# A graph-attention kernel: weights transposed first, a shorter last table store, and weighing steps moved among the logits steps near the end

## The chip, the cores and the metric

One core of a Trainium2 chip runs the kernel. The metric is the time of one execution on the device in microseconds (us), the median of several runs. Engines: TensorE (PE, with PEld for its weight loads), VectorE (DVE), ScalarE (ACT), GpSimd (POOL), SyncE (SP). An engine works through its instructions in the order in which the program emits them and waits on semaphores for the others. SP, ACT and POOL also issue DMAs, on queues named SPq, ACTq and POOLq.

## The reference

3125 nodes with 128 features, 100000 edges sorted by destination, five edge types `r`, eight heads of 16. For each type, an edge's logit per head is query times key, the softmax runs over the edges of that type into one node, and the values are summed with it:

```python
q = einsum('eh,khd->ekd', x_dst, W_Q[r]); k = ...x_src, W_K[r]; v = ...x_src, W_V[r]
logits = (q * k).sum(-1) / scale + attn_bias[r]
masked = where(mask, logits, NEG)
exp_l = where(mask, exp(masked - segment_max(masked, dst)[dst]), 0.0)
out += segment_sum((exp_l / (segment_sum(exp_l, dst)[dst] + 1e-12))[:, :, None] * v, dst)
# after the types
h = out @ out_proj_w.T + out_proj_b + x
x = layernorm(x + layernorm(h) * ln_gamma + ln_beta)
```

Only the edges of type `r` count for `r`, so every edge is worked on once, with the weights of its own type.

## The kernel before, in words

The nodes lie in 25 blocks of 128 (the last has 53), the edges in 196 groups of 512. A group is a tile of 128 partitions by 4 edges, and its edges go to at most 25 neighbouring nodes, that is 125 rows (node, type) of a window. The whole work is in `windowed_path`; `general_path` is a fall-back for other inputs and does not run here. The Tile framework is told to keep the order in which instructions are emitted (`manual_schedule`), so the order of the Python code is the order of each engine's queue.

**Start.** Weights, node features and edge lists are loaded. The first node of each group (`fr`) is copied to floats (`frf`), spread to all partitions by a matmul with `ones` (`fp`, `firsts`) and turned into `first`, `first5` and part of `nkey`. Then the weights are transposed on PE in four quarters (`d0` = 0, 4, 8, 12) into two PSUM buffers `wp`, and copied out to `wkv` and `wq` by DVE and ACT. A loop over the 25 blocks makes the table of keys and values: `turn(b)` transposes a block of features, `table(b)` multiplies it with `wkv` (three matmuls), copies the result to one of three buffers `kvs` and stores it to `kv_d` in DRAM, 128 nodes x 5 types x 256 floats, 640 KB. Between tables the loop runs the pieces in `side`: `rows_of` finds the rows of the edge list in which a node's edges begin, `in_row` fetches them (POOL), `count` counts (ACT), `keys_a` to `keys_c` and `along` build the indices, `checks` tests the input's form.

**Steps.** The rest is one loop over steps `k`, written as a hand-made software pipeline. Per group: `gather` fetches the 512 table rows with four indirect DMAs on POOL into one of 24 buffers `kv`; `fetch` loads the group's keys `kt` and window of queries `qw` (SP); `spot` makes a one-hot matrix `hot` (DVE); `spread_q` brings the queries to the edges (12 bf16 matmuls); `logits` multiplies and reduces (DVE, lines 613 and 614); `store_logits` writes them to `lg_d`. At step `k` group `k` has its logits.

Once all edges of a block have logits, `maxima_load` fetches, for each node, 64 edges from the block's place in `lg_d` into `ell` (one indirect DMA on POOL), and `maxima` (ACT copies `ell` to `by_head`, DVE adds masks and reduces) works out the maxima in two parts, three types and then two; `store_m` writes them. From `LAG` = 8 steps after the block's last logits on, its groups can be weighed: `fetch_m`, `spread_m` (12 small matmuls, `me`), `less_max` (DVE), `exps` (ACT), `weigh` (DVE, line 707), `places` (ACT: the one-hots `at` of destinations, five Abs at line 719 and one Relu at line 722), `sums` (PE, fp32, lines 733 to 743), `carry` (ACT), `norm` (DVE), `by_node` (ACT). The table `at_k` gives the step in which a group `v` is weighed:

```python
for v in range(NGR):
    k = max(k + 1, full_at(block_of(v), D) + LAG)
    at_k[v] = k
```

It runs 19 steps behind the logits from `v` = 22 on. So logits end at step 195, and steps 196 to 214 hold weighing only. When a block is complete, `project` (PE) and `residual` (DVE) come at `done_at` and one step later, `roots` (a square root on ACT, which needs another activation table than the exponential) at `done_at` + 2 and `norms` (DVE) a step after that; `store_z` writes the block. `fetch_x` loads the residual's input `xr`; for the last, smaller block it first clears the buffer on DVE. The steps of blocks 19 to 24: roots at 186, 194, 201, 209, 217 and 220, the last normalisation at 222. Maxima of blocks 22, 23 and 24 are at steps 187/188, 195/196 and 198/199.

POOL's queue: gathers are emitted up to `AHEAD` = 3 groups ahead of the step, and a block's logits load follows the gathers of its step. SP's queue in each step: `fetch`, `fetch_x`, `store_z`, `store_m`, `store_q`, `fetch_m`, then `store_logits`.

Of the kernel before, what the change touches and what calls it, by code (L numbers as in the profile page):

```python
# [17 lines left out]
P = 128  # L18
# [3 lines left out]
R = 5  # L22
# [24 lines left out]
WR = WN * R  # L47
RH = 3
# [67 lines left out]
def windowed_path(  # L116
# [9 lines left out]
    kv_d = dram.tile([NP * R, KVW], F32, name="kv_d")  # L126
# [108 lines left out]
    five = iota("five", [[R, WN]], WN, mult=-1)  # L235
    ones = keep("ones", [P, P])
    nc.vector.memset(ones, 1.0)
    eps_t = keep("eps_t", [P, 1])
    nc.vector.memset(eps_t, LN_EPS)
# [14 lines left out]
    for b in range(NT):  # L254
# [4 lines left out]
    frf = load.tile([1, NGR + NSR], F32, name="frf")  # L259
    nc.vector.tensor_copy(frf, fr)  # L260
    fp = pps.tile([P, NGR + NSR], F32, name="fp", tag="tr", bufs=2)
    nc.tensor.matmul(fp, ones[0:1, :], frf, start=True, stop=True)
    firsts = load.tile([P, NGR + NSR], F32, name="firsts")
    nc.vector.tensor_copy(firsts, fp)
    nc.vector.tensor_copy(first, frf[:, :NGR])
    nc.vector.tensor_scalar_mul(first5, frf[:, :NGR], float(R))
    nc.vector.tensor_tensor(
        nkey[:, T, 1:], firsts[:, 1:NGR], firsts[:, : NGR - 1], op=ALU.subtract
    )
    nc.vector.tensor_scalar(  # L270
        nkey[:, T, 1:], nkey[:, T, 1:], float(R), row_of, op0=ALU.mult, op1=ALU.subtract
    )
    grp = load.tile([P, NT], F32, name="grp")
    grp_i = load.tile([P, NT], I32, name="grp_i")
    nodeh = load.tile([P, NT], F32, name="nodeh")
    nc.vector.tensor_scalar_add(nodeh, node, -0.5)
    into = load.tile([P, NT], F32, name="into")


# [3 lines left out]
    for d0 in range(0, HD, 4):  # L283
        wp = pps.tile([P, 4, 3, R, HEADS], F32, name="wp", tag="wp", bufs=2)
        for d in range(4):
            nc.tensor.transpose(
                wp[:, d].rearrange("h s r k -> h (s r k)"), wn[:, d0 + d :: HD],
                ident[: 3 * R * HEADS, : 3 * R * HEADS],
            )
        for s, (copy, to) in enumerate(  # L290
            ((nc.vector.tensor_copy, kv_to[:, 0]), (nc.scalar.copy, kv_to[:, 1]),
             (nc.vector.tensor_copy, q_to))
        ):
            copy(to[:, :, :, d0 : d0 + 4], wp[:, :, s].rearrange("h d r k -> h r k d"))

# [8 lines left out]
    def table(b, xT):  # L304
        kvs = work.tile([P, R * 2, H], F32, name="kvs", bufs=3)
        wf = wkv.rearrange("h r s c -> h (r s) c")
        for n, (c0, c1) in enumerate(((0, 4), (4, 8), (8, 10))):
# [9 lines left out]
            kv_d[b * P * R : (b + 1) * P * R, :].rearrange("(p r) c -> p (r c)", r=R),  # L317
            kvs.rearrange("p s h -> p (s h)"),
# [113 lines left out]
    def checks():  # L432
# [18 lines left out]
        0: [lambda: rows_of(0, 5)],  # L451
        1: [lambda: rows_of(5, 10)],
        2: [lambda: rows_of(10, 15)],
# [18 lines left out]
    for b in range(NT):  # L472
# [5 lines left out]
        while len(rows) < min(NT, 5 * b + 5) and len(rows) - counted < 8:  # L478
            rows[len(rows)] = in_row(len(rows))
# [53 lines left out]
    def fetch_x(name, b):  # L533
        n = min(P, N - b * P)
        xb = flow.tile([P, H], F32, name=name, bufs=2)
# [178 lines left out]
    def places(g):  # L714
# [3 lines left out]
        for t in range(n):  # L718
            nc.scalar.activation(  # L719
                at[:, t, :], row_at[:, :WR], AF.Abs, bias=nkey[:, t, g : g + 1], scale=1.0  # L720
            )
        nc.scalar.activation(at[:, :n, :], at[:, :n, :], AF.Relu, bias=1.0, scale=-1.0)  # L722
# [56 lines left out]
    def pair():  # L779
        return late_flow.tile([P, 2, nc.vector.BN_AGGR_DIM], F32, name="mv", bufs=2)  # L780
# [6 lines left out]
    def residual(b):  # L787
# [6 lines left out]
        h = late_flow.tile([P, H], F32, name="h")  # L794
# [9 lines left out]
    def norms(b):  # L804
        sd, mv = live.pop(("sd", b)), live.pop(("mv", b))
        nc.vector.reciprocal(sd, sd)
        if b < NT:
# [9 lines left out]
            live["mv", b + 1] = nxt = pair()  # L817
            nc.vector.memset(nxt, 0.0)
# [15 lines left out]

    at_k, k = {}, 0
    for v in range(NGR):
        k = max(k + 1, full_at(block_of(v), D) + LAG)
        at_k[v] = k
    v_at = {k: v for v, k in at_k.items()}
    done_at = {b: at_k[full_at(b)] + 4 for b in range(NT)}  # L840
    for b in range(1, NT):
        done_at[b] = max(done_at[b], done_at[b - 1] + 1)
    done_at[NT] = done_at[NT - 1] + 2
    norm_at = {b: d + (3 if b < NT - 1 else 2) for b, d in done_at.items()}

    q_at = [
        min(g for g in range(NGR) if min(block_of(g) + 1, NT - 1) >= b) - 3 for b in range(NT)
    ]
    q_from = []
    for b in range(NT):  # L850
        f = q_at[b] - 7
# [28 lines left out]
    for k in range(done_at[NT] + 4):  # L880
        v = v_at.get(k)
        q_step = {k - f: b for b, f in enumerate(q_from) if b not in first_b and -2 <= k - f <= 5}

        if k + 3 < NGR:
            fetch(k + 3)
        if -2 in q_step:
            fetch_x("xq", q_step[-2])
        for b in range(NT):
            if done_at[b] - 1 == k:
                fetch_x("xr", b)  # L890
            if norm_at[b + 1] + 1 == k:
                store_z(b)
            if full_at(b, D) + LAG - 3 == k:
# [3 lines left out]
        for u in range(NGR):  # L897
            if max(at_k[u] - 3, full_at(block_of(u), D) + LAG - 2) == k:
                fetch_m(u)

        while gathered < min(k + AHEAD, NGR - 1):
            gathered += 1
            gather(gathered)
        for b in range(NT):
            if full_at(b, D) + 1 == k:
# [20 lines left out]
        if k + 1 < NGR:  # L926
            spread_q(k + 1)
# [4 lines left out]
        if k + 1 < NGR:  # L932
            types(k + 1)
        if k < NGR:
            logits(k)
            store_logits(k)
# [4 lines left out]
        if k + 2 < NGR:  # L941
            spot(k + 2)
        if v_at.get(k + 1) is not None:
            places(v_at[k + 1])
# [4 lines left out]
        for b in range(NT):  # L949
            if full_at(b, D) + LAG - 5 == k:  # L950
                maxima(b, 0, RH)
            if full_at(b, D) + LAG - 4 == k:
                maxima(b, RH, R)
        for b in range(NT + 1):
            if done_at[b] + 2 == k:
                roots(b)
            if norm_at[b] == k:
# [514 lines left out]
```

## Time and profile before

| | |
|---|---|
| median of 3 runs | 1222.6 us (1218.9 to 1222.96) |
| profiled execution | 1219.8 us, its span 1218.0 us |
| busy, share of the span | PE 810.3 us (67%), PEld 701.4 (58%), DVE 928.8 (76%), ACT 750.5 (62%), POOL 804.9 (66%) |
| first and last gather, start | 100.3 and 1113.6 us |
| last logits, last weighing, start | 1118.8 and 1200.5 us |
| mean granted TensorE clock | 0.765 |

The profile is one execution. A slice row shows an engine's busy share in 40 equal parts of the span. A row of a timeline gives start and duration in us, engine, line, operation, tiles and shapes, how many rows were merged, and in brackets how long the engine was idle before and what ended that. In the window tables come the busy times of PE, PEld, DVE, ACT and POOL with counts, then the clock, the DMA engines' share and GB/s.

### The profile page before, as it was taken

The numbers are of one execution on the slowest core, as the hardware profiler recorded it, in microseconds if no ns is written. First come the engines' busy times: TensorE is split into PE (matmuls) and PEld (weight loads), VectorE is DVE, ScalarE is ACT, GpSimd is POOL, SyncE is SP. The second block draws the span as 40 slices with busy tenths as digits, with TensorE's granted clock in tenths as the row PEclk, the third lists the DMA queues.
The fourth block names the chain that finished last, engine by engine and source line by source line (L and its number), as shares of the span: only waits on it lengthen the run. The fifth ranks groups of instructions, "written<-read, shape, count | busy, mean of one in ns | idle before, by whom it ended". The sixth has DMA issues, their size and how long they took to land.

```text
span 1218.0 us, 25296 instructions
## 1 busy us (share of the span) xinstructions
PE 810.3 (67%) x7503; PEld 701.4 (58%) x7503; DVE 928.8 (76%) x2478; ACT 750.5 (62%) x2488; POOL 804.9 (66%) x902
## 2 busy tenths in 40 slices
PE   4793446657667766776667667766776686568584
PEld 2451235547656665665566656665665675567484
DVE  4751376777887898888888988888888889778744
ACT  1661015447656766776677667756766676667594
POOL 2705777777777777777777777777777777775000
PEclk9996566677777887887687778778877878777566
DMA  6984787667666767776776677667766776665000
GB/s 146 361 329 153 211 208 183 155 170 192 167 166 181 184 167 173 180 181 167 180 185 169 172 176 194 174 161 183 189 165 169 179 183 165 173 159 128 8 8 14
DMA packets 181138, 207.33 MB, mean 170 GB/s; under 512 B 82614, under 2 KB 145871, under 8 KB 180872
## 3 DMA queue, kind: packets, MB, share of 16 engines
q0 software_dynamic: 41392, 116.59, 34.5%
q1 hardware_dynamic: 135176, 84.34, 28.1%
q10 hardware_dynamic: 4424, 4.71, 1.5%
q8 instruction: 61, 1.00, 0.3%
q14 instruction: 85, 0.70, 0.2%
HBM read 169.90 MB, written 35.62 MB: 169 GB/s over the span
## 4 chain that ended last, share of the span: by engine, by line
DVE 31%; DMA 20%; POOL 14%; PE 13%; issue 11%; ACT 10%; SPq 1%; DVEq 0%; ACTq 0%; POOLq 0%
POOL kv L527 14%; DMA kv<-kv_d,idx 10%; DMA ell<-lg_d,start_i 5%; DVE prod L613 4%; DVE lg L614 4%; DVE wv L707 4%; PE pp L733 4%; DVE wl L653 3%; ACT at L719 3%; PE pr L309 3%; DVE mx L659 2%; DVE hot L591 2%; PE qe L600 2%; DVE den L756 1%; PE prq L553 1%
## 5 line engine op out<-in xcount | busy, mean ns | idle before, releaser
L527 POOL DMA_INDIRECT kv<-kv_d,idx x784 | 746.3, 952 | 274.2 <-issue 195.1
L733 PE MATMUL pp<-wv,at 128*125 128x136 f32 x1568 | 307.9, 354 | 17.0 <-DVE o L758 14.9
L719 ACT ACTIVATE at<-row_at,nkey 128x125 f32<-128x125 f32 x979 | 305.1, 390 | 0.0
L733 PEld LDWEIGHTS pp<-wv,at 128*125 128x125 f32 x1568 | 261.6, 243 | 25.4 <-DVE o L758 16.9
L600 PE MATMUL qe<-qw,hot 125*128 125x128 bf16 x2352 | 210.9, 254 | 31.1 <-DMA qw<-q_d 15.3
L600 PEld LDWEIGHTS <-hot 125*128 125x128 bf16 x2352 | 197.4, 124 | 36.8 <-DVE hot L591 21.4
L690 PE MATMUL me<-mw,hot 125*128 125x8 bf16 x2352 | 91.6, 168 | 184.5 <-DVE wv L707 116.0
L690 PEld LDWEIGHTS <-hot 125*128 125x128 bf16 x2352 | 84.3, 102 | 224.0 <-DVE wv L707 124.6
L707 DVE TENSOR_TENSOR wv<-kv,me 128x512 f32<-128x512 f32 x196 | 133.3, 680 | 76.1 <-ACT wv L702 74.0
L701 ACT ACTIVATE me<-me 128x32 f32<-128x32 f32 x196 | 36.3, 185 | 226.9 <-DVE me L697 225.8
L613 DVE TENSOR_TENSOR prod<-kv,qe 128x512 f32<-128x512 f32 x196 | 134.1, 684 | 33.7 <-PE qe L600 17.3
L722 ACT ACTIVATE at<-at 128x625 f32<-128x625 f32 (+1 forms) x196 | 142.2, 726 | 6.2
L614 DVE TENSOR_REDUCE lg<-prod 128x32 f32<-128x512 f32 x196 | 134.4, 686 | 6.8
L737 PE MATMUL pp<-pt,at 125*125 125x136 f32 x390 | 103.3, 355 | 33.9 <-ACT pt L749 33.7
L553 PE MATMUL prq<-wq,xTq 128*128 128x384 f32 (+1 forms) x100 | 59.4, 691 | 78.4 <-DVE rem L563 77.2
L737 PEld LDWEIGHTS pp<-pt,at 125*125 125x125 f32 x390 | 79.1, 246 | 41.2 <-ACT pt L749 40.6
L591 DVE TENSOR_SCALAR hot<-kt,row_of 125x512 bf16<-125x512 bf16 x196 | 73.5, 375 | 13.6 <-DMA kt<-key_d 13.4
L653 DVE TENSOR_TENSOR wl<-by_head,shut 128x1536 f32<-128x1536 f32 (+1 forms) x50 | 74.5, 1491 | 10.7 <-ACT by_head L638 9.8
L743 PEld LDWEIGHTS pp<-rsum,o 125*128 125x128 f32 x392 | 80.6, 250 | 1.7 <-ACT oT L768 1.4
L659 DVE TENSOR_REDUCE mx<-wl 128x24 f32<-128x1536 f32 (+1 forms) x50 | 74.3, 1486 | 1.7
L553 PEld LDWEIGHTS prq<-wq,xTq 128*128 128x128 f32 x100 | 22.6, 281 | 87.7 <-DVE rem L563 85.6
L743 PE MATMUL pp<-rsum,o 125*128 125x25 f32 x392 | 72.0, 267 | 1.4 <-DVE xr L537 1.3
(156 smaller groups left out, 992.9 us busy)
## 6 DMA issues: line engine op xcount, KB each, us to landing
kt<-key_d SPq DMA_DIRECT2D x196, 128.0 KB
qw<-q_d SPq DMA_DIRECT2D x196, 96.0 KB
kv_d<-kvs SPq DMA_DIRECT2D x25, 640.0 KB
kv<-kv_d,idx POOLq DMA_INDIRECT x784
q_d<-q SPq DMA_DIRECT2D x25, 480.0 KB
lg_d<-lg SPq DMA_DIRECT2D x196, 18.0 KB
mw<-m_d SPq DMA_DIRECT2D x196, 6.0 KB
xq<-in_x SPq DMA_DIRECT2D x24, 64.0 KB
```

The lines of the kernel that those rows point to most:

```text
L527: nc.gpsimd.indirect_dma_start(out=kv[:, t, :], out_offset=None, in_=kv_d[:, :], in_offset=bass.IndirectOffsetOnAxis(ap=idx[:, t, g : g + ...
L600: nc.tensor.matmul(qe[:, t, :], hot[:, t, :], qw[:WR, s, :], start=(s == 0), stop=(s == 2))
L613: nc.vector.tensor_tensor(prod, kv[:, :, :H], live.pop(("qe", g)), op=ALU.mult)
L614: nc.vector.tensor_reduce(lg[:, :, :HEADS], prod.rearrange("p t (k d) -> p t k d", d=HD), AX.X, ALU.add)
L653: nc.vector.tensor_tensor(wl[:, :n], by_head[:, None].to_broadcast([P, n, HEADS, D]), shut[:, :n, None, :].to_broadcast([P, n, HEADS, D]), ...
L690: nc.tensor.matmul(me[:, t, :], hot[:, t, :], mw[:WR, s, :], start=(s == 0), stop=(s == 2))
L707: nc.vector.tensor_tensor(wv[:, :, :H].rearrange("p t (k d) -> p t k d", d=HD), kv[:, :, H:].rearrange("p t (k d) -> p t k d", d=HD), live ...
L719: nc.scalar.activation(at[:, t, :], row_at[:, :WR], AF.Abs, bias=nkey[:, t, g : g + 1], scale=1.0)
L722: nc.scalar.activation(at[:, :n, :], at[:, :n, :], AF.Relu, bias=1.0, scale=-1.0)
L733: nc.tensor.matmul(pp, at[:, t, :], wv[:, t, :], start=(t == 0), stop=(t == T - 1 and g == 0))
L737: nc.tensor.matmul(pp, at[:WR, T, :], live.pop(("pt", g - 1)), start=False, stop=True)
L743: nc.tensor.matmul(op, live.pop(("o5", done)), rsum[:WR], start=True, stop=True)
```

## The change

At the start, the weights' transposes come before the work on `frf`, which becomes a function `begins` and runs after the first table; the row searches move one table later. The copies of a quarter go to one engine, DVE for `d0` = 0 and 8, ACT for 4 and 12. The last table store writes 64 partitions instead of 128, and `kv_d` ends there.

Near the end, five groups (`CATCH_UP`) take two steps each: the second has no logits, only weighing. So the last logits are at step 200 (`final`), while `at_k` stays as it was. From block 22 on the lag is 6 steps; the maxima come at steps 185/186, 196/197 and 201/202. From step 184 on gathers are emitted one step ahead. From step 199 on three of the five one-hot slices of `at` are made by DVE with a comparison, and ACT's Relu covers the rest. Norms are emitted in the step of their roots. Roots that would fall between steps 199 and 214 are put behind the last weighing: blocks 21, 22 and 23 at 215, 216 and 217; 24 and the last normalisation stay at 220 and 222. To hold them, `xr`, `mv` and `h` get four buffers.

```diff
+CATCH_UP = (186, 188, 190, 192, 194)
...
-        for s, (copy, to) in enumerate(
-            ((nc.vector.tensor_copy, kv_to[:, 0]), (nc.scalar.copy, kv_to[:, 1]),
-             (nc.vector.tensor_copy, q_to))
-        ):
+        copy = nc.vector.tensor_copy if d0 % 8 == 0 else nc.scalar.copy
+        for s, to in enumerate((kv_to[:, 0], kv_to[:, 1], q_to)):
...
+    def begins():
+        nc.vector.tensor_copy(frf, fr)
+        fp = pps.tile([P, NGR + NSR], F32, name="fp", tag="tr", bufs=2)
+        nc.tensor.matmul(fp, ones[0:1, :], frf, start=True, stop=True)
+        nc.vector.tensor_copy(firsts, fp)
...
+        n_ = P if b < NT - 1 else 64
...
         nc.sync.dma_start(
-            kv_d[b * P * R : (b + 1) * P * R, :].rearrange("(p r) c -> p (r c)", r=R),
-            kvs.rearrange("p s h -> p (s h)"),
+            kv_d[b * P * R : (b * P + n_) * R, :].rearrange("(p r) c -> p (r c)", r=R),
+            kvs[:n_].rearrange("p s h -> p (s h)"),
         )
...
-        0: [lambda: rows_of(0, 5)],
-        1: [lambda: rows_of(5, 10)],
-        2: [lambda: rows_of(10, 15)],
+        0: [begins],
+        1: [lambda: rows_of(0, 5)],
+        2: [lambda: rows_of(5, 10), lambda: rows_of(10, 15)],
...
-        while len(rows) < min(NT, 5 * b + 5) and len(rows) - counted < 8:
+        while len(rows) < min(NT, 5 * b) and len(rows) - counted < 8:
...
-    def places(g):
+    def places(g, on_dve):
...
+            if t < on_dve:
+                nc.vector.tensor_scalar(
+                    at[:, t, :], row_at[:, :WR], nkey[:, t, g : g + 1], 0.0,
+                    op0=ALU.add, op1=ALU.is_equal,
+                )
+            else:
...
-        nc.scalar.activation(at[:, :n, :], at[:, :n, :], AF.Relu, bias=1.0, scale=-1.0)
+        nc.scalar.activation(
+            at[:, on_dve:n, :], at[:, on_dve:n, :], AF.Relu, bias=1.0, scale=-1.0
+        )
...
+    for g in range(NGR):
+        step_of[g] = n
+        n += 2 if g in CATCH_UP else 1
+    group_at = {k: g for g, k in step_of.items()}
+    final = step_of[NGR - 1]
...
+        return LAG if b < NT - 3 else LAG - 2
+    full_step = [step_of[full_at(b, D)] for b in range(NT)]
+    ready = [full_step[b] + lag(b) for b in range(NT)]
...
-        k = max(k + 1, full_at(block_of(v), D) + LAG)
+        k = max(k + 1, ready[block_of(v)])
...
-    norm_at = {b: d + (3 if b < NT - 1 else 2) for b, d in done_at.items()}
+    root_at = {b: d + 2 for b, d in done_at.items()}
+    for b in range(NT):
+        if final - 1 <= root_at[b] <= last_k:
+            root_at[b] = max(last_k, root_at[b - 1]) + 1
+    root_at[NT] = root_at[NT - 1] + 2
...
-        while gathered < min(k + AHEAD, NGR - 1):
+        while gathered < NGR - 1 and step_of[gathered + 1] <= k + (AHEAD if k < final - 16 else 1):
...
-            places(v_at[k + 1])
+            places(v_at[k + 1], 3 if k >= final - 1 else 0)
...
         for b in range(NT + 1):
-            if done_at[b] + 2 == k:
+            if root_at[b] == k:
                 roots(b)
-            if norm_at[b] == k:
                 norms(b)
```

In the step loop `k < NGR` and group numbers are replaced by `group_at`, and the maxima, their stores and loads go by `ready` instead of `full_at(b, D) + LAG`.

## The prediction

> **What bounds the kernel now.** I read the page first (slices, costliest groups), then the timelines of SP and POOL around the first gather, then busy time by window, then the timelines of DVE, ACT and PE from 1040 us to the end.
>
> ```profile
> span 1218.0 us, 25296 instructions
> ...
> POOL 2705777777777777777777777777777777775000
> ...
> PEclk9996566677777887887687778778877878777566
> ...
> L527 POOL DMA_INDIRECT kv<-kv_d,idx x784 | 746.3, 952 | 274.2 <-issue 195.1
> ```
>
> POOL shows the same 7 from slice 5 to slice 36: 784 gathers of 0.95 us with 0.30 us of issue between them, one per 1.25 us, without a hole from 100.3 to 1114.6 us. Three stages follow: before the gathers (100 us), the gathers (1014 us at a pace that nothing else sets), and what is left after them (103 us). The change touches the first and the last.
>
> ```profile
> 58.81 0.69 DVE L315 COPY kvs<-pr 128x512 f32<-128x512 f32 x1 [2.12 <-DMA kv_d<-kvs]
> ...
> 95.25 0.32 SPq L316 DMA_DIRECT2D kv_d<-kvs  x1
> ...
> 100.31 0.94 POOL L527 DMA_INDIRECT kv<-kv_d,idx  x1 [35.52 <-DMA bias<-in_L_gnn_attn_bias]
> ```
>
> The first gather reads the whole table, so it follows the last table store. The view names the bias load, which landed at about the same time; nothing in the code makes a gather wait for it. The row at 58.81 is a stall in the middle of the table loop: a copy waits for a buffer whose store has not landed.
>
> ```profile
> 1049.00:1119.00 70.00, 48.82 (x505) 45.42 (x505) 58.67 (x156) 44.87 (x160) 50.66 (x54) 0.71 0.63 153
> 1119.00:1166.00 47.00, 27.82 (x206) 25.91 (x205) 31.74 (x92) 29.85 (x93) 0.94 (x1) 0.61 0.06 13
> 1166.00:1201.00 35.00, 31.32 (x262) 29.72 (x260) 17.82 (x67) 33.00 (x116) 0.00 (x0) 0.64 0.05 10
> ```
>
> Columns: PE, weight loads, DVE, ACT, POOL, clock, DMA. In the last window only weighing is left: ACT is busy 94%, PE 89% at a clock of 0.64.
>
> ```profile
> 1047.95 1.07 ACT L638 COPY by_head<-ell 128x512 f32<-128x512 f32 x1 [3.02 <-DMA ell<-lg_d,start_i]
> ...
> 1120.25 0.33 SPq L619 DMA_DIRECT2D lg_d<-lg  x1
> 1122.56 0.94 POOL L626 DMA_INDIRECT ell<-lg_d,start_i  x1 [6.57 <-ACT wv L702]
> ...
> 1159.08 1.28 ACT L801 ACT_TABLE_LOAD   x1
> 1160.93 1.28 ACT L701 ACT_TABLE_LOAD   x1
> 1162.65 0.69 DVE L707 TENSOR_TENSOR wv<-kv,me 128x512 f32<-128x512 f32 x1 [4.26 <-ACT wv L702]
> ...
> 1190.23 2.18 PE L733 MATMUL pp<-wv,at 128*125 128x136 f32 x8 [0.25 <-DVE o L758]
> 1193.68 2.18 PE L733 MATMUL pp<-wv,at 128*125 128x136 f32 x8 [0.24 <-DVE o L758]
> ...
> 1208.86 0.28 DVE L793 TENSOR_TENSOR xr<-xr,beta_t 53x128 f32<-53x128 f32 x1 [0.75 <-DMA xr<-in_x]
> ```
>
> The first row is the last place where compute waits for POOL (block 21's logits). From there to the end compute is behind the gathers (logits of group 188 start 13.3 us after its last gather was issued), so the end is a sum of compute steps. A free full step takes 2.92 us (logits at 1059.79, 1062.69), a weighing-only step 2.75 us (weighings at 1168.86, 1171.61, 1174.37).
>
> **The step counts.** Worked out from the code: before, logits end at step 195, weighing at 214, the program at 223. After, five idle logits steps put the last logits at step 200; the last weighing stays at 214, the end at 223. So five weighing steps change places, none disappears: by itself that is worth 0, since the stretch they go into is compute-bound too. What counts is what the move makes wait, and what goes from the end.
>
> **Before the gathers.** *Half store:* issue to first gather is 5.06 us; its packets run from 96.28 to 98.99 us, 2.7 us for 640 KB beside four small loads, and POOL starts 1.3 us after the last. Half the rows: between 0 and -1.4; I take **-1.2**. *Weights first:* the weights' last packet is at 9.3 us, but ACT issues loads until 16.33 and loads its table until 17.64, and now copies two of the four quarters whole. The first table matmul comes at about 20.4 instead of 21.9 (-1.3). Against it, `begins` (about 2.1 us of DVE and a matmul, today beside the weight wait at 13 to 17 us) goes onto DVE, which is busy without a hole from 25.6 to 48 us, and the row searches behind it start some 2.6 us later, their POOL reads too. DVE reaches table 8 about 1.1 us later. The stall at 58.81 (PE idle nearly 3 us) covers that: the bytes ahead of it are the same. I take **0**, between -1.5 and +2.5; without the cover it would be +1.1. Whatever it is passes 1:1 through the gathers.
>
> **Steps up to 184: 0.** Late gathers and loads keep their order. Norms now sit in the step of their roots, so DVE waits some 1.5 us for the square root where today it first goes on; the 3.0 us wait for block 21's logits covers it. Without the cover: under 0.5 us a block.
>
> **Steps 185 to 203.** POOL: looking ahead by one step puts block 22's logits load before gathers 187 and 188; POOL then waits about 2 us for the store of logits 184, and gathers run 8 to 14 us ahead, so nobody notices. Block 23's load comes before gathers 194 and 195 and waits for logits 192. From the rows at 1120.25 and 1122.56: logits start to load start 3.8 us, landing 3.35 us later (packets to 1125.84), 7.15 in all. ACT could take it 5.85 us after the logits began: **+1.3**. Behind it on POOL, gather 194 lands some 12 us after logits 192 began; its logits need it after 20. Block 24's load waits in the same way for logits 195, with less before it: **+1.8**. SP: block 22's maxima are stored two steps earlier, 23's one later, 24's three later, all before their first reader.
> Roots: block 19's two table loads now fall beside block 22's second maxima (4.2 us of DVE) instead of ahead of a weighing: **-2.7**. Block 21's go to the end: today 5.76 + 3.45 us for two steps of 2.75, **-3.7**. One-hots on DVE: three operations of 0.15 to 0.19 us (nearest row: 128x128 at 0.18); in steps 200 and 202, where DVE is the bound, **+1.0**; in step 199 ACT sheds 1.5 us and DVE's own 2.4 us bound: **-0.35**. Sum **-2.65**.
>
> **Steps 203 to 214**, 34.4 us today. Block 22's roots go: **-3.7**. Sharing one-hots takes ACT from 2.75 to some 1.5 us a step; DVE then needs 2.4 (weighing wait 0.65, weighing 0.61, normalising 0.72, one-hots 0.45). Late next is PE: the rows at 1190.23 and 1193.68 show it at half clock, its period 3.01 us without a root between (1170.57 to 1173.59), 1.95 at full. The Trainium skill's "TensorE: Matmul & The Clock Gate", Part 1, says activity releases the gate: after a busy window of 3.4 us the array runs at full clock. By that rule a denser PE would speed up and the 11 steps fall to 2.4 us (-3.9). The trace speaks against it: from 1181.2 to 1198.3 the granted clock is 0.5 while PE is busy five sixths of the time. At 72% of half clock the step is 2.84 (+1.0). Between -3.9 and +1.0 I take 2.7 us, near the 2.75 that stands: **-0.55**.
>
> On the table loads: the skill's "ScalarE: Activation LUTs", "What ACT_TABLE_LOAD costs", counts a drain and gives 2.66 us a switch, 5.3 for the pair. The trace has two of 1.283 and a root of 0.295: the weighing at 1162.65 comes 5.75 us after the one before, 3.0 more than 2.75. By the rule two roots fewer are worth 4.6 us more; I use the rows.
>
> **The end.** Roots and norms of 21 and 22 (1.5 us of DVE each) now come after the last weighing, with one table load in all, beside other chains. But the memset ahead of the last `xr` load follows 22's norms in DVE's queue: it moves from 1205.75 to about 1207.6, SP first stores a finished block, and the load (2.9 us) ends at 1210.95 instead of 1208.86. The last block waits for it already: **+2.1**, at least +0.5 (block 23's residual behind 21's norms).
>
> **Sum**: -1.2 + 0 - 2.65 - 3.7 - 0.55 + 2.1 = -6.0 us, on a profiled execution of 1219.8 us (span 1218.0 and 1.8 around it): 1213.8. That execution is one of the quick ones; from the median of 1222.6 the same sum gives 1216.6. I give **1215.0**.
>
> **Rivals.** *No change (0.28), about 1221.* Compute merely changes places, ACT's savings turn into PE time at half clock (+1.0 instead of -0.55), and the logits loads land as late as in the crowded stretch (5.9 instead of 3.35 us, twice): -6.0 + 1.5 + 5.1 = 0.6. For: the step counts; 72% of half clock. Against: DMA is nearly idle there.
> *Slower (0.12), about 1229.* The weighing steps put their fp32 matmuls among full steps, and PE is granted half clock throughout. A full step's PE work at half clock is 3.0 + 1.4 = 4.4 us instead of 2.92: eight more such steps among 187 to 200 cost 8 x 1.5 = 12 us. It decides once the clock there falls under about 0.6. For: steps of 3.97 and 4.38 us at 1102 to 1113. Against: clock 0.71 today, and each weighing step has less PE work than the one it parts.
> *More (0.15), about 1208.* Full clock in the last steps (-3.3 more), the start gaining its whole 1.3, the last `xr` load costing 0.5 only: -6.0 - 3.3 - 1.3 - 1.6 = -12. Against: the clock row.
>
> **Numbers.** Forecast case 0.45, its own range 1210 to 1220. A measurement of this kernel can tell about 0.5% (6 us) from no change, that is below 1216.5 faster: 0.8 of the forecast case and all of "more", 0.51; slower 0.12; the same 0.37. The 8-in-10 range is 1206 to 1226.
>
> **What would show it.** First gather at 99.1 (over 101: weights first costs). One square-root table load after the last logits instead of three. POOL holes ahead of the last two logits loads. First weighing of block 24's stretch with DVE idle for `ell` 1 to 2 us. Weighing steps of 2.4 us mean that the clock rose, 3.0 that PE took over; a span above 1222 at an early first gather means full steps at half clock.

## The result and the profile after

The changed kernel takes 1215.3 us (median of 6 runs, 1214.33 to 1218.6), the kernel before, beside it, 1220.5 (6 runs). The ratio is 0.9959, its 95% interval 0.9942 to 0.9976: 0.4% faster, about 5 us. The forecast was 1215.0 us within 1206 to 1226; the gain itself lies inside the 0.5% that the prediction called "the same", on the edge to "faster". The profiled execution has a span of 1212.5 us where before had 1218.0.

The page of the changed kernel, the rows shown of before:

```profile
span 1212.5 us, 25279 instructions
...
POOL 2714777777777777777777777777777777774200
...
PEclk9996565778679776877988787878777888768767
...
L530 POOL DMA_INDIRECT kv<-kv_d,idx x784 | 745.4, 951 | 275.6 <-issue 195.7
```

The gathers keep their pace (0.951 us and 0.30 of issue). The new 4 and 2 near the end of POOL's row are a hole of 14.8 us, in which POOL waits to issue block 23's logits load, and the last eight gathers, which now stand behind that load.

Four marks cut the span into what the prediction summed: the start of weighing 163, 184 and 195 on DVE, and the end of DVE's last instruction. Times in us:

| | before | after | difference | predicted |
|---|---|---|---|---|
| first gather | 100.31 | 101.63 | +1.32 | -1.2 |
| weighing 163 | 1061.10 | 1060.06 | -1.04 | -1.2 |
| from there to weighing 184 | 105.00 | 102.87 | -2.13 | -2.65 |
| to weighing 195 | 34.39 | 29.55 | -4.84 | -4.25 |
| to the last DVE instruction | 12.15 | 14.57 | +2.42 | +2.1 |
| sum | | | -5.59 | -6.0 |

So the sum and the three terms of the end came out within 0.6 us. The first term did not: the first gather is later, and what was lost there was regained on the way to weighing 163. That this stretch came out near its forecast (-1.04 for -1.2) is chance: e1 below shows that the changed start is worth nothing that can be told.

The start, in the timelines of DVE, SP's queue and POOL of the changed kernel:

```profile
57.09 0.69 DVE L318 COPY kvs<-pr 128x512 f32<-128x512 f32 x1 [1.09 <-DMA kv_d<-kvs]
...
60.15 0.69 DVE L318 COPY kvs<-pr 128x512 f32<-128x512 f32 x1 [2.16 <-DMA kv_d<-kvs]
...
70.41 0.69 DVE L318 COPY kvs<-pr 128x512 f32<-128x512 f32 x1 [2.13 <-DMA kv_d<-kvs]
...
96.70 0.52 SPq L319 DMA_DIRECT2D kv_d<-kvs  x1
...
101.63 0.94 POOL L530 DMA_INDIRECT kv<-kv_d,idx  x1 [36.94 <-DMA bias<-in_L_gnn_attn_bias]
```

The first table matmul comes at 18.4 instead of 21.9 us, sooner than forecast, but the lead is all but gone at the fourth table store (36.71 instead of 36.92). Later, where before waited for a table store at 58.81 and 71.11 (3.7 us), three copies now wait, for 5.4 us in all.

The end, in the timelines of DVE, POOL, ACT and SP's queue of the changed kernel:

```profile
1115.41 0.17 DVE L817 RECIPROCAL sd<-sd 128x2 f32<-128x2 f32 x1 [2.52 <-ACT sd L812]
...
1117.00 0.68 DVE L616 TENSOR_TENSOR prod<-kv,qe 128x512 f32<-128x512 f32 x1
...
1120.67 0.94 POOL L629 DMA_INDIRECT ell<-lg_d,start_i  x1 [14.78 <-ACT lg L610]
...
1124.24 0.33 DVE L643 SCALAR_TENSOR_TENSOR mine<-slot,deg,ell 128x64 f32<-128x64 f32 x1 [2.12 <-DMA ell<-lg_d,start_i]
...
1143.10 0.29 DVE L806 TENSOR_TENSOR h<-pj,xr 128x128 f32<-128x128 f32 x1 [1.79 <-PE pj L787]
...
1143.94 0.69 DVE L616 TENSOR_TENSOR prod<-kv,qe 128x512 f32<-128x512 f32 x1
...
1147.72 0.94 POOL L629 DMA_INDIRECT ell<-lg_d,start_i  x1 [16.03 <-DMA mw<-m_d]
...
1151.06 0.33 DVE L643 SCALAR_TENSOR_TENSOR mine<-slot,deg,ell 128x64 f32<-128x64 f32 x1 [1.35 <-DMA ell<-lg_d,start_i]
...
1165.47 0.69 DVE L710 TENSOR_TENSOR wv<-kv,me 128x512 f32<-128x512 f32 x1 [0.47 <-ACT wv L705]
1168.02 0.69 DVE L710 TENSOR_TENSOR wv<-kv,me 128x512 f32<-128x512 f32 x1 [0.47 <-ACT wv L705]
...
1193.41 1.28 ACT L812 ACT_TABLE_LOAD   x1
...
1200.28 0.33 SPq L541 DMA_DIRECT2D xr<-in_x  x1
...
1203.28 0.28 DVE L804 TENSOR_TENSOR xr<-xr,beta_t 53x128 f32<-53x128 f32 x1 [1.70 <-DMA xr<-in_x]
```

Most signs that the prediction named are there: POOL's holes ahead of the last two logits loads (14.78 us at 1120.67, 16.03 at 1147.72), DVE idle for `ell` (2.12 and 1.35 us), and one square-root table load after the last logits (1193.41) where before had three. The last `xr` is issued at 1200.28 and waited for. One sign pointed the wrong way: a first gather over 101 us was to mean that the new order of the start costs time, and e1 and e2 don't bear that out. Weighing steps are 2.55 us apart; DVE is busy in all of it but the 0.47 us in which ACT makes the weights, so DVE sets them.

### The profile page after: what moved, and what is told of

The parts are those of the page before. It is cut to its first block, busy times and chain, and to the rows that moved or that the text cites. A ratio compares the mean times of both kernels' runs of the same rounds, so it can differ in the third digit from the quotient of the medians.

```text
span 1212.5 us, 25279 instructions
## 1 busy us (share of the span) xinstructions
PE 799.7 (66%) x7503; PEld 690.8 (57%) x7503; DVE 936.2 (77%) x2521; ACT 728.9 (60%) x2441; POOL 801.9 (66%) x902
## 4 chain that ended last, share of the span: by engine, by line
DVE 34%; DMA 22%; PE 14%; issue 10%; POOL 9%; ACT 9%; SPq 1%; DVEq 0%; ACTq 0%; POOLq 0%
DMA kv<-kv_d,idx 9%; POOL kv L530 9%; DMA ell<-lg_d,start_i 6%; DVE lg L617 5%; DVE prod L616 5%; DVE wv L710 4%; PE pp L744 4%; DVE wl L656 4%; PE pr L312 3%; ACT at L728 3%; DVE mx L662 2%; PE prq L556 2%; PE qe L603 2%; DVE hot L594 2%; DMA kt<-key_d 2%
## 5 line engine op out<-in xcount | busy, mean ns | idle before, releaser
L744 PE MATMUL pp<-wv,at 128*125 128x136 f32 x1568 | 300.6, 348 | 18.0 <-DVE o L769 15.9
L728 ACT ACTIVATE at<-row_at,nkey 128x125 f32<-128x125 f32 x934 | 292.0, 390 | 0.0
L744 PEld LDWEIGHTS pp<-wv,at 128*125 128x125 f32 x1568 | 255.1, 237 | 26.9 <-DVE o L769 18.3
L603 PE MATMUL qe<-qw,hot 125*128 125x128 bf16 x2352 | 208.3, 252 | 29.6 <-DVE hot L594 14.6
L603 PEld LDWEIGHTS <-hot 125*128 125x128 bf16 x2352 | 195.2, 124 | 35.4 <-DVE hot L594 22.7
L693 PEld LDWEIGHTS <-hot 125*128 125x128 bf16 x2352 | 83.2, 101 | 222.3 <-DVE wv L710 134.7
L731 ACT ACTIVATE at<-at 128x625 f32<-128x625 f32 (+2 forms) x196 | 137.5, 702 | 6.2
L748 PE MATMUL pp<-pt,at 125*125 125x136 f32 x390 | 100.6, 347 | 35.3 <-ACT pt L760 35.3
```

What stands on the lines that cost most here:

```text
L603: nc.tensor.matmul(qe[:, t, :], hot[:, t, :], qw[:WR, s, :], start=(s == 0), stop=(s == 2))
L693: nc.tensor.matmul(me[:, t, :], hot[:, t, :], mw[:WR, s, :], start=(s == 0), stop=(s == 2))
L728: nc.scalar.activation(at[:, t, :], row_at[:, :WR], AF.Abs, bias=nkey[:, t, g : g + 1], scale=1.0)
L731: nc.scalar.activation(at[:, on_dve:n, :], at[:, on_dve:n, :], AF.Relu, bias=1.0, scale=-1.0)
L744: nc.tensor.matmul(pp, at[:, t, :], wv[:, t, :], start=(t == 0), stop=(t == T - 1 and g == 0))
L748: nc.tensor.matmul(pp, at[:WR, T, :], live.pop(("pt", g - 1)), start=False, stop=True)
```

## The experiments

Each profile gives the first gather and the lengths of the three parts of the end, weighing 163 to 184, 184 to 195 and 195 to the last DVE instruction. Their sum is the end stage. Ratios are to the kernel before, on the same chip, with their 95% intervals.

| run | median us | ratio | first gather | 163-184 | 184-195 | tail | end stage |
|---|---|---|---|---|---|---|---|
| before | 1220.5 | | 100.31 | 105.00 | 34.39 | 12.15 | 151.5 |
| after | 1215.29 | 0.9959 (0.9942-0.9976) | 101.63 | 102.87 | 29.55 | 14.57 | 147.0 |
| e1 start only | 1219.63 | 1.0001 (0.9985-1.0017) | 101.65 | 105.32 | 34.45 | 12.22 | 152.0 |
| e2 old start | 1213.71 | 0.9947 (0.9932-0.9962) | 102.48 | 102.31 | 29.83 | 14.74 | 146.9 |
| e3 `begins` first | 1212.28 | 0.9940 (0.9922-0.9957) | 100.29 | 101.85 | 30.90 | 15.16 | 147.9 |
| e4 roots back | 1216.23 | 0.9969 (0.9958-0.9980) | 100.52 | 102.04 | 31.73 | 12.13 | 145.9 |
| e5 one-hots on ACT | 1216.39 | 0.9964 (0.9951-0.9977) | 101.47 | 102.70 | 30.74 | 15.00 | 148.4 |
| e6 no catch-up | 1209.81 | 0.9914 (0.9895-0.9932) | 100.45 | 98.80 | 30.02 | 15.31 | 144.1 |
| e7 `xr` early | 1213.24 | 0.9955 (0.9934-0.9976) | 103.33 | 101.36 | 30.11 | 12.78 | 144.3 |
| e8 gathers 3 ahead | 1218.67 | 0.9980 (0.9965-0.9995) | 105.55 | 104.32 | 29.76 | 14.53 | 148.6 |
| e9 norms in step | 1218.11 | 0.9981 (0.9970-0.9992) | 102.30 | 102.36 | 34.77 | 12.24 | 149.4 |
| e10 lag back | 1215.24 | 0.9956 (0.9943-0.9970) | 102.69 | 91.62 | 38.94 | 14.43 | 145.0 |
| e11 best | 1210.75 | 0.9912 (0.9896-0.9927) | 104.74 | 97.53 | 29.57 | 13.21 | 140.3 |
| e12 best, `begins` first | 1206.98 | 0.9885 (0.9870-0.9900) | 98.43 | 98.49 | 30.62 | 12.80 | 141.9 |

Two things are to be read first. The first gather varies from profile to profile: nine kernels with the changed start have it anywhere between 100.45 and 105.55 us (median 101.65). From the first gather to weighing 163 all profiles take 957 to 962 us. So one profile says little about the start, while the end stage repeats to 1 or 2 us (before and e1, which have the same end: 151.5 and 152.0; after, e2 and e3: 147.0, 146.9, 147.9). Inside it, the step from weighing 165 to 166 takes 5.4 to 8.8 us in kernels with the same code there (after, e2 to e5, e7), and after, with 8.4, is at the slow end. So the end is judged by the end stage and, where 1 or 2 us matter, by the steps that an edit touches; the start is judged by ratios.

### The start: e1, e2, e3

e1 is the kernel before with the changed start, that is the hunks ahead of `fetch_x`, nothing else. In part:

```diff
+        n_ = P if b < NT - 1 else 64
...
-        0: [lambda: rows_of(0, 5)],
-        1: [lambda: rows_of(5, 10)],
-        2: [lambda: rows_of(10, 15)],
+        0: [begins],
+        1: [lambda: rows_of(0, 5)],
+        2: [lambda: rows_of(5, 10), lambda: rows_of(10, 15)],
```

> The kernel before with the change's start alone (weights first, `begins` after the first table, row searches one table later, half a last store). In the changed kernel's trace the first table matmul came 3.5 us earlier (18.4 for 21.9) and yet the first gather 1.3 us later (101.63 for 100.31). Theory A (the delayed row searches and `begins` hold the table loop, so the start part costs): first gather again at 101 to 102, time +0 to +1.5 us on the kernel before, about 1221. Rival B (that 1.3 us is scatter of the stores in that one profile): first gather at 99 to 100, time 1219. Prediction's own step (weights first 0, half store -1.2): first gather 99.1.

Measured: ratio 1.0001, first gather 101.65. The changed start is worth nothing that can be told, 0 within 2 us. The first gather is where A put it, but e4 and e6, with the same start, have it at 100.5, so that alone decides nothing.

e2 is the changed kernel with the start of before, but half a last store. In part:

```diff
-        0: [begins],
-        1: [lambda: rows_of(0, 5)],
-        2: [lambda: rows_of(5, 10), lambda: rows_of(10, 15)],
+        0: [lambda: rows_of(0, 5)],
+        1: [lambda: rows_of(5, 10)],
+        2: [lambda: rows_of(10, 15)],
```

> The changed kernel with the old start (the work on `frf` before the weights, searches where they were, copies shared as before), but half a last store. Theory A: first gather at about 99.1 (100.3 less the 1.2 of the half store), 2.5 us before the changed kernel's, and the time 1 to 2.5 us lower, about 1213 to 1214. Rival B (scatter): first gather anywhere between 99 and 101.5, time as the changed kernel, 1215.3. The end stage must be that of the changed kernel: last weighing to last DVE instruction 14.6 us, weighing steps 2.55 us.

Measured: 1213.7, ratio 0.9947 beside the changed kernel's 0.9959, which is no difference, and a first gather at 102.48. Rival B in substance: the old start does not bring an earlier first gather or a shorter time, so the changed kernel's later one was scatter. The half store's 1.2 us is not there either.

e3 keeps the weights first but calls `begins` at once:

```diff
+    begins()
+
     grp = load.tile([P, NT], F32, name="grp")
...
-        0: [begins],
-        1: [lambda: rows_of(0, 5)],
-        2: [lambda: rows_of(5, 10), lambda: rows_of(10, 15)],
+        0: [lambda: rows_of(0, 5)],
+        1: [lambda: rows_of(5, 10)],
+        2: [lambda: rows_of(10, 15)],
...
-        while len(rows) < min(NT, 5 * b) and len(rows) - counted < 8:
+        while len(rows) < min(NT, 5 * b + 5) and len(rows) - counted < 8:
```

> The changed kernel with `begins` called right after the weights' copies, in the time in which DVE waits for the first transposed features, and the row searches in tables 0 to 2 as before. Theory A (the row searches set the loop): first table still at about 18.5 to 19.5 us, first gather 98 to 99.1, time about 1213. Rival C (the loop is set by the table stores, that is by the DMA engines, and starting it sooner only moves the stall): first table as early, but first gather not before 99.5, time 1214 to 1215.

Measured: 1212.3, ratio 0.9940, first gather 100.29. Alone this is within its interval of the changed kernel; with e12 beside e11 (0.9885 for 0.9912, first gather 98.43) it is the second pair that gains some 2 to 3 us, so what e3 puts back probably did cost. e3 moves `begins` and the row searches together; the windows of the table loop and the fourth table store (SP's queue) point to `begins`. Before:

```profile
8.00:25.00 17.00, 9.25 (x25) 5.39 (x26) 4.93 (x18) 3.04 (x6) 0.33 (x9) 1.00 0.70 154
25.00:50.00 25.00, 21.17 (x63) 10.73 (x62) 22.65 (x43) 15.09 (x37) 16.44 (x15) 1.00 0.80 291
50.00:75.00 25.00, 22.52 (x83) 12.84 (x82) 11.93 (x21) 19.16 (x52) 11.34 (x11) 1.00 1.00 397
...
36.92 0.32 SPq L316 DMA_DIRECT2D kv_d<-kvs  x1
```

After:

```profile
8.00:25.00 17.00, 11.05 (x30) 6.16 (x31) 4.24 (x16) 3.52 (x9) 0.33 (x9) 1.00 0.79 176
25.00:50.00 25.00, 19.92 (x57) 9.91 (x56) 22.65 (x44) 14.30 (x35) 15.86 (x15) 0.93 0.78 276
50.00:75.00 25.00, 22.92 (x81) 13.12 (x80) 10.37 (x20) 19.18 (x51) 10.38 (x11) 0.93 0.96 374
...
36.71 0.32 SPq L319 DMA_DIRECT2D kv_d<-kvs  x1
```

e12, with `begins` first:

```profile
8.00:25.00 17.00, 12.52 (x31) 6.85 (x32) 6.25 (x19) 3.60 (x10) 0.35 (x9) 1.00 0.76 158
25.00:50.00 25.00, 20.29 (x65) 10.21 (x64) 21.77 (x43) 15.19 (x38) 18.89 (x16) 1.00 0.86 316
50.00:75.00 25.00, 22.95 (x80) 12.46 (x80) 12.06 (x21) 19.39 (x53) 10.05 (x10) 1.00 0.99 393
...
34.17 0.32 SPq L321 DMA_DIRECT2D kv_d<-kvs  x1
```

The last columns are DMA share and GB/s. From 50 to 75 us the DMA engines have next to no room (shares of 0.96 to 1.00), so rival C's bound is real: a table begun early gains little there. What an early start can gain is bytes moved before 50 us. GB/s times us makes, from 8 to 50 us, 9.9 MB both before and after: the changed kernel moves more at first (176 for 154 GB/s) and less then (276 for 291). Its first table's lead of 3.5 us goes for the most part on DVE, which does `begins` from 22.8 to 25.6 us and then, as in before, is busy 22.65 of 25 us. With `begins` in DVE's idle time the lead is still 2.8 us at the fourth store, and 10.6 MB are moved. All profiles together say the same: the two latest first gathers (e8, e11) stand after 8.9 MB, the two earliest (e12, e3) after 10.6 and 10.9. Why the same start moves 8.9 MB in one execution and 10.0 in another stays open.

### What the catch-up steps cost: e6, e8, e10

e6 takes out the five weighing-only steps and the shorter lag:

```diff
-CATCH_UP = (186, 188, 190, 192, 194)
+CATCH_UP = ()
...
-        return LAG if b < NT - 3 else LAG - 2
+        return LAG
...
-        if final - 1 <= root_at[b] <= last_k:
+        if 199 <= root_at[b] <= last_k:
...
-        while gathered < NGR - 1 and step_of[gathered + 1] <= k + (AHEAD if k < final - 16 else 1):
+        while gathered < NGR - 1 and step_of[gathered + 1] <= k + AHEAD:
...
-            places(v_at[k + 1], 3 if k >= final - 1 else 0)
+            places(v_at[k + 1], 3 if k >= 199 else 0)
```

> The changed kernel without the five weighing-only steps and without the shorter lag: logits end at step 195, maxima of blocks 22 to 24 at steps 187/188, 195/196 and 198/199 as before, gathers three ahead; late roots, shared one-hots from step 199 and the new start stay. By the prediction's terms the five steps brought 2.7 us (block 19's root hidden) and cost 3.1 (two waits for block logits): without them -0.4 us, 1215. Rival F: a weighing-only step between full steps takes 2.14 us on DVE where one at the end takes 2.55 to 2.75, so the five steps bring another 2 us: without them +1.6 to +2.5 us, about 1217. Rival G (the moved maxima cover root 21 and the catch-up is what pays): +4 us, 1219.

Measured: 1209.8 us, ratio 0.9914 against 0.9959: the kernel is faster without them, by 0.45% (0.25% either way, from the two intervals); the end stage is 2.9 us shorter and 163 to 184 alone 4.1. F and G, which had the catch-up pay, are both wrong. e6's DVE timeline:

```profile
1079.17 0.17 DVE L817 RECIPROCAL sd<-sd 128x2 f32<-128x2 f32 x1 [1.57 <-ACT sd L812]
...
1116.95 0.17 DVE L817 RECIPROCAL sd<-sd 128x2 f32<-128x2 f32 x1 [1.83 <-ACT sd L812]
...
1122.28 1.76 DVE L656 TENSOR_TENSOR wl<-by_head,shut 128x1536 f32<-128x1536 f32 x1 [0.42 <-ACT by_head L641]
...
1138.40 1.76 DVE L656 TENSOR_TENSOR wl<-by_head,shut 128x1536 f32<-128x1536 f32 x1 [1.10 <-ACT by_head L641]
```

No wait for `ell` is left, and block 19's root (the first row), which the prediction gave 2.7 us of exposure, costs 1.57. Between weighings 165 and 184 DVE is idle 25.0 us before, 22.0 after and 17.8 in e6, at 73.1, 74.0 and 74.1 us of work: of the 4.2 us between after and e6, the two waits for `ell` are 3.5; the other gaps go both ways (the wait for `pj` at 1143.10 is gone, ACT's copies of `ell` are waited for a little longer). The other profiles repeat it: from weighing 163 to 184 the kernels with the catch-up as made (after, e2, e3, e7) take 101.4 to 102.9 us, those without it (e6, e11, e12) 97.5 to 98.8, and in the former the two waits for `ell` are 3.3 to 3.5 us.

e10 keeps the catch-up and gives the lag back:

```diff
-        return LAG if b < NT - 3 else LAG - 2
+        return LAG if b != NT - 2 else LAG - 1
```

> The changed kernel with the catch-up steps kept, but the lag back at 8 steps for blocks 22 and 24 and 7 for block 23; no weighing moves by it, the maxima come two, one and two steps later (187/188, 197/198, 203/204). Theory K (the catch-up costs because each of the last two logits loads is asked for in the very step, or the step before, that needs it): DVE's waits for `ell`, 2.12 and 1.36 us, fall to under 0.5 each, block 19's root is exposed again (1.6 us): -1 to -2 us in the end stage (147.0 to 145 or 146), time 1213 to 1214. Rival L (what costs is the late last logits and PE in the dense stretch, `pj` 1.8 us): the waits go but others take their place, 147, 1215.

```profile
1080.81 0.17 DVE L817 RECIPROCAL sd<-sd 128x2 f32<-128x2 f32 x1 [1.68 <-ACT sd L812]
...
1125.49 0.69 DVE L616 TENSOR_TENSOR prod<-kv,qe 128x512 f32<-128x512 f32 x1 [1.67 <-PE qe L603]
...
1155.15 1.76 DVE L656 TENSOR_TENSOR wl<-by_head,shut 128x1536 f32<-128x1536 f32 x1 [0.46 <-DVE shut L651]
```

In its DVE timeline the waits for `ell` are gone, block 19's root is exposed again (1.68 us) and PE is a little late once (1.67). The end stage is 145.0: some 2.0 of the 2.9 us are the shorter lag, as K had it. The times don't resolve it (0.9956 for 0.9959), and 2 us of one profile's end stage can be scatter, so K rests on the waits that are gone. The last 0.9 us is no more than the scatter of the stage; whether it is PE, as in L, or the gathers, which e10 still holds back, is not settled. (Since the maxima move, 163 to 184 and 184 to 195 can be compared only as a sum.)

e8 issues the gathers three steps ahead to the end:

```diff
-        while gathered < NGR - 1 and step_of[gathered + 1] <= k + (AHEAD if k < final - 16 else 1):
+        while gathered < NGR - 1 and step_of[gathered + 1] <= k + AHEAD:
```

> The changed kernel with gathers three steps ahead to the end. Prediction: nobody notices when the gathers are issued there, so the time stays, 1215; gathers 194 and 195 are issued before block 23's logits load and POOL's queue is empty when that load can start; the load's landing is 0 to 0.5 us sooner. Rival I: block 22's load waits behind two more groups of gathers (5 us later), ACT's copy of it and block 22's first maxima wait for it at step 185: +1 to +3 us.

```profile
1081.39 0.33 DVE L643 SCALAR_TENSOR_TENSOR mine<-slot,deg,ell 128x64 f32<-128x64 f32 x1 [4.82 <-DMA ell<-lg_d,start_i]
```

Rival I: block 22's first maxima wait 4.82 us for a load that stands behind more gathers, the step from weighing 166 to 167 is 12.1 us instead of 7.4, the end stage 1.6 us longer and the ratio 0.9980. With a lag of six steps, the gathers must be held back. The prediction was right that nobody misses the late gathers; it did not say that without it the shorter lag would not work.

### Roots, norms, one-hots, the tail: e4, e5, e7, e9

e4 leaves the roots two steps behind the sums:

```diff
-        if final - 1 <= root_at[b] <= last_k:
-            root_at[b] = max(last_k, root_at[b - 1]) + 1
+        root_at[b] += 0
```

> The changed kernel with the roots of blocks 21, 22 and 23 back at two steps after their sums (steps 201, 209 and 217). Prediction's terms: 3.7 us for each of roots 21 and 22, less 2.1 to 2.4 us of the tail that they made longer: +5 us, 1220. Rival D (root 21 now falls beside block 24's first maxima and is hidden as block 19's was; only root 22 counts): +3.7 less 2.4, +1.3, about 1216.5. In the trace: the step of weighing 190 (root 22) 5.8 us in both; the one of weighing 182 5 to 6 us more by the first, under 1 us more by the second.

Measured: ratio 0.9969 beside 0.9959, no difference. From weighing 182 to 183, where root 21 falls, it is 10.03 us instead of 8.55; from 190 to 191, with root 22, 4.77 instead of 2.54; the tail falls from 14.57 to 12.13. So a root costs 1.5 to 2.2 us here, not 3.7, and the tail takes most of it back. The end stage, 145.9, is 1.1 us shorter than with late roots, but that lies ahead of weighing 182, in steps that this edit does not touch. From weighing 182 to the end e4 takes 60.6 us, and after, e2, e3 and e8, which have the same code there, 59.3, 59.9, 61.4 and 59.5: late roots bring about 0.5 us on the mean, inside that scatter. D's time (1216.5) fits the median; of its reasons, root 21 is not hidden and root 22 is smaller than it had.

e9 changes one line of the kernel before:

```diff
-    norm_at = {b: d + (3 if b < NT - 1 else 2) for b, d in done_at.items()}
+    norm_at = {b: d + 2 for b, d in done_at.items()}
```

> The kernel before with one edit: each block's norms are emitted in the step of its root instead of a step later. Theory J (found in the experiments: DVE then does 1.5 us of norms while ACT loads the exponential's table back, where it used to sit idle): the two steps around a root cost 1.3 to 1.5 us less, for the four roots 19 to 22 that lie in compute-bound steps; from weighing 163 to the last DVE instruction 151.5 us becomes about 146, time about 1215. Prediction's step (the wait for the root is moved, not saved; up to 0.5 us worse for a block): 1220 to 1222.

```profile
1080.73 0.17 DVE L806 RECIPROCAL sd<-sd 128x2 f32<-128x2 f32 x1 [0.91 <-ACT sd L801]
...
1118.32 0.17 DVE L806 RECIPROCAL sd<-sd 128x2 f32<-128x2 f32 x1 [1.83 <-ACT sd L801]
1118.55 1.28 ACT L701 ACT_TABLE_LOAD   x1
```

DVE now waits for the root itself (rows above, from its timeline), but not for ACT's second table load (the row at 1118.55, from ACT's), which runs under the 1.5 us of norms. The two steps around root 19 fall from 14.72 to 12.81 us, around root 20 from 13.86 to 12.58, around roots 21 and 22 from 9.21 to 8.70; against that, the step of block 22's residual grows by 0.9 us, and other steps scatter. The end stage is 149.4, 2.2 us shorter, and the ratio 0.9981, which is 2.3 us (1.0 to 3.7). Theory J has the mechanism, at half its size in all; the prediction's step had the wrong sign.

e5 keeps the one-hots on ACT:

```diff
-            places(v_at[k + 1], 3 if k >= final - 1 else 0)
+            places(v_at[k + 1], 0)
```

> The changed kernel with all five one-hots of every step on ACT. The steps 203 to 214 took 29.6 us (2.55 each, DVE-bound) in the changed kernel. Theory A: they go back to 2.75 (ACT-bound), +2.2 us, and steps 199 to 202 lose the 0.7 us that the one-hots cost DVE where it was the bound, so the end stage is +1.2 to +2.2 us, time about 1217. Rival E (PE at half clock was the bound all along and the shared one-hots gave nothing): the last steps stay at 2.55 to 2.6, time 1215.

Measured: steps of 2.75 again, 184 to 195 longer by 1.2 us, end stage +1.4; the times (1216.4) can't tell it, and the stage alone can't either (e3 has 30.90 us with shared one-hots), so it is the steps that speak for theory A. What is left of PE shows in e3's profile, in its windows:

```profile
1165.00:1187.00 22.00, 19.41 (x185) 18.62 (x183) 16.60 (x70) 13.49 (x56) 0.00 (x0) 0.73 0.06 10
1187.00:1195.00 8.00, 8.00 (x59) 8.00 (x59) 4.92 (x22) 3.89 (x18) 0.00 (x0) 0.50 0.00 0
```

In the second stretch PE is busy all 8 us at a clock of 0.50, and the weighings there are 3.02 us apart (1188.79, 1191.81, 1194.83): rival E's bound holds for stretches only, not for all steps. Single steps of 2.94 to 3.02 us stand in most profiles with shared one-hots.

e7 fetches the last `xr` nine steps earlier:

```diff
-            if done_at[b] - 1 == k:
+            if (done_at[b] - 1 if b < NT - 1 else last_k - 6) == k:
                 fetch_x("xr", b)
```

> The changed kernel with the last block's `xr` cleared and loaded at step 208 instead of 217. Prediction's step (the clear behind norms(22) holds the last load, +2.1 us): the 1.70 us wait of DVE for `xr` goes, last weighing to last DVE instruction 14.6 becomes 12.9 us, time 1213.5. Rival H (the store of the last sums, project and the norms hold the last block as long): the wait moves to PE's `pj` or ACT's root, gain under 0.5 us.

```profile
1200.61 0.32 DVE L837 TENSOR_SCALAR z<-y,mv,sd 128x128 f32<-128x128 f32 x1
1200.84 0.28 DVE L804 TENSOR_TENSOR xr<-xr,beta_t 53x128 f32<-53x128 f32 x1
```

The wait is gone (no bracket in the second row): tail 12.78, 1.8 us less, the forecast step and its size. The end stage is shorter by 2.7 us; what goes beyond the 1.8 comes from before weighing 184, ahead of this edit. The median is 2.0 us lower, the ratios can't tell.

### The parts that pay, together: e11, e12

e11 is e6 with e7's edit; e12 is e11 with e3's.

> Without the catch-up steps and the shorter lag, and with the last block's `xr` loaded at step 208: the two gains added. End stage 144.1 less 2.1 to 2.5 of tail = 141.6 to 142, time about 1208. Rival (in the tail the last block's sums, project or root end as late): 143.5 to 144, 1210.

> As e11_best, with `begins` right after the weights' copies and the row searches one table earlier, as in e3. If the start is limited by the table stores, the same as e11_best within 1.5 us (scatter of the first gather: 100.3 to 102.5 in most profiles so far); if the searches matter, 1 to 2 us less, 1206 to 1207.

e11: end stage 140.3, 1.3 us better than expected, but a profile whose first gather comes at 104.74; the ratio of 0.9912 can't be told from e6's. e12: 1207.0 us, ratio 0.9885 (0.9870 to 0.9900), 14 us faster than before and some 8 us than the change as made. It is the fastest version of this study.

## Why the prediction was right, and where it was not

*The total* was right: -5.6 us in the profile for -6.0 forecast, 1215.3 for 1215.0. It fell into "the same" by the measured 0.41%, to which 0.37 was given, and not into "faster" with 0.51. It was right partly by luck: several terms were off and cancelled. The start gave nothing where 1.2 us were summed, and the end gave 4.5 of its 4.8 us with terms that were off both ways.

*Half store, -1.2.* Mis-sized. From the end of the last copy to the first gather it is 5.09 and 5.11 us with a whole store (before, e9) and 4.80 to 5.58 in the twelve profiles with half of one, 4.98 on the mean: 0.1 us. The sum halved the packets' time. But SP takes 0.52 us for the issue instead of 0.32 (96.70 and 95.25 in the timelines), its packets start 1.5 us after that instead of 1.0, and from the first to the last they take 2.1 us where the whole store's took 2.7. Why the issue is slower was not tried.

*Weights first, 0.* Right in amount (e1: 0 within 2 us), with the reason in part. The lead was 3.5 us and not 1.3, `begins` took 2.8 us of DVE, with its wait for PE, and not 2.1, so lead and cost were even by the fourth table, ahead of the stall that was to cover them. The stall is real: a DMA share of 1.00 from 50 to 75 us in before says that the bytes set the pace there. The claim that the start passes 1:1 through the gathers stands within the scatter, 957 to 962 us from first gather to weighing 163; before's own profile was towards the slow end of that (960.8, after 958.4), which made up for its early first gather.

*The two logits loads, +1.3 and +1.8.* Right in mechanism and nearly in size: from the start of the logits to the landing of the load it is 7.2 and 7.1 us (1117.00 to 1124.24, 1143.94 to 1151.06) where 7.15 was worked out, DVE idle 2.12 and 1.35 us. These waits are what the catch-up with its shorter lag costs, and most of why e6 beats the change.

*Block 19's root, -2.7; norms in the step of the root, 0.* Two terms that belong together. With the norms in its step, root 19 holds DVE for 1.57 us (e6) where 2.7 was summed, and that move pays also where no maxima cover the root: -1.9 at root 19 and -1.3 at root 20 in e9, -0.5 in weighing steps. The failed step is "without the cover: under 0.5 us a block" as a loss: it saw that DVE waits for the root, not that the table load back then runs beside the norms. In e6 these gains stand without the catch-up.

*Late roots 21 and 22, -3.7 each.* Right against the kernel before, too much against the changed one. Root 22's 3.7 us are 3.2 once the norms sit in its step (e9) and 2.2 beside shared one-hots (e4); root 21, beside block 24's maxima, is 1.5; and the tail's 2.4 cancels most. The sum counted the same idle time twice, as what a root costs and as what the other edits fill.

*One-hots on DVE, steps of 2.7.* 2.55. The prediction weighed the clock-gate rule (steps of 2.4) against the half clock seen in before (2.84). In most steps neither ended last: DVE did. The clock of before was itself in part chance. e1 has the same code from weighing 184 to 195, and its row stands below that of before:

```profile
1166.10:1200.49 34.39, 30.87 (x259) 29.38 (x259) 17.31 (x66) 32.77 (x113) 0.00 (x0) 0.63 0.06 10
...
1165.87:1200.33 34.46, 28.25 (x258) 26.51 (x258) 17.32 (x67) 32.83 (x113) 0.00 (x0) 0.76 0.05 10
```

A clock of 0.63 or 0.76, and the same 34.4 us, with ACT busy 95%: there ACT set the steps, not PE, and the 0.78 of the changed kernel from 1163 to 1193 us is no effect of the edit that can be told. With shared one-hots the clock does matter: e3, with 0.67 over these steps, takes 30.9 us for after's 29.6. There PE is busy without a break for 8 us at half clock, which speaks against a plain reading of the rule that the prediction cites.

*The last `xr`, +2.1.* Right: tail +2.42, and e7 gets 1.8 of it back.

*Rivals.* "No change" named the right forces (half clock, logits loads), too strong. "Slower", with PE at half clock throughout the full steps, did not happen: the changed kernel's clock is 0.75 from 1049 to 1119 us, where before had 0.71.

## What to carry to other kernels

When a step schedule is shuffled in a compute-bound stretch, count the steps between the one that issues a load and the one that needs what it brings: here the shorter lag made them the same step, and that cost more than the shuffle hid. Work that an engine has anyway (here the norms) can be put right where the other engine reloads its table; by itself that was worth 2.3 us. Before a term like "half the bytes" or "one root less" enters a sum, ask what else fills the same idle time, and judge it by the stage it lies in: the stage lengths repeated within 1 or 2 us where whole times and first gathers scattered by more, and below that the steps themselves have to be compared. A clock read from one profile is one draw.

## What the runs showed of the hardware

A store of 64 partitions was hardly quicker to land than one of 128 (4.98 us on the mean from last copy to first gather, for 5.10): its issue took 0.52 us instead of 0.32 and its first packet came 0.5 us later. PE ran 8 us at a granted clock of 0.50 while busy all the time (e3, 1187 to 1195 us), and at 1.00 in the less busy stretch of the changed kernel from 1173 to 1178 us (3.58 of 5 us), so in these stretches more work did not bring more clock. With the same code the clock over eleven weighing steps was 0.63 in one execution (before) and 0.76 in another (e1).
